# Between layers 1 and 2 of a four-layer sparse graph network: which engine takes roots and norms, in which order the vector work stands, and how the last rows are scaled for layer 3

## The chip, the core and the metric

The kernel runs on one core of one Trainium2 chip. A core has five engines with queues of their own: PE (TensorE, matrix products; PEld is its weight load), DVE (VectorE), ACT (ScalarE), POOL (GpSimd, which here also issues the indirect DMAs) and SP (SyncE, which issues the plain DMAs). Each engine works through its queue in order. What is measured is the device time of one execution in microseconds (us), as the median of several runs.

## What is computed

`x` has 2708 rows of 512 float32 numbers, and `adj` is a 2708 x 2708 matrix with about 0.15% of its entries non-zero, plus its diagonal. Four layers follow one another, each `x = layernorm(x + layer(x, adj))`. The change touches the end of layer 1, the whole of layer 2's scaling, and the way from layer 2 to 3:

```python
# layer 2
mask = incidence_m > 0
head = mask.astype(incidence_m.dtype)
head = head / jnp.maximum(jnp.sqrt(jnp.sum(head * head, axis=-1, keepdims=True)), EPS)
inc = incidence_m + head
edge_fea = inc @ cur
edge_degree = jnp.sum(inc, axis=-1, keepdims=True)
return edge_fea / edge_degree
...
# layer 3
A = adj_matrix + jnp.eye(n, dtype=adj_matrix.dtype)
deg = jnp.sum(A, axis=0)
d = deg ** (-0.5)
d = jnp.where(jnp.isinf(d), 0.0, d)
A = d[:, None] * A * d[None, :]
Hm = A @ H
out = jnp.tanh(Hm @ W.T + b)
```

So layer 2 needs, for every row, one over the root of its count of non-zeros (`inv_norm`) and its row sum; layer 3 needs one over the root of every column sum (`d_inv`), and its gathered rows are already multiplied by it: what layer 3 reads is `y = d_inv * x`.

## The kernel before

The rows are cut into 24 blocks of 113 (the last has 109; `NB`, `R`, `rows(i)`). During layer 0 the kernel finds the non-zeros of each block and keeps them as lists of 4 x 128 edges (`EC` = 4 chunks): source row, row in the block, value. From then on a product `adj @ x` of one block is: four indirect DMAs (`gather`, L600, issued by POOL, 128 rows of 512 numbers each) bring the source rows from a table in HBM to one of three buffers `gath[i % 3]`, and four matrix products (`aggregate`, L613) multiply them by a 128 x 113 spread matrix `s`, which `values` (L1291) makes on DVE. For layer 2 `incidence` (L1564, L1567) makes from `s` the matrix `inc2`. A float32 product appears in the trace as two PE passes.

Each layer ends a block with a layernorm and writes the new rows to the table that the next layer gathers from (`move_rows`, two DMAs on SP): `table[1]` from `norm1`, `table[2]` from `norm2`. A row may be needed by any block, so the first gather of layer 2 waits for the last block's write of `table[1]`, and the first gather of layer 3 for the last write of `table[2]`. PSUM pools are opened anew between the layers (`phase.close()`).

The order of the instructions on every engine is the order of the code: the scheduler is switched off (`manual_schedule`). Around the change that order is, for the last block of layer 1 (i = 23): products `l1s` (`sums1`) and `l1e` (`scored_sums1`); the transpose that brings the column sums in (`source_sums_in`, L1518, with its copy on ACT, L1519); transposes of the first two rows of `inv_norm` (`turn_norm`, L1551); the gates on ACT (`gates1`, L1427, L1428); `gated1` on DVE (L1434 to L1440); the norm of block 22 (`norm1`, L1484, L1487, and its two writes); the loads of layer 3's bias row and of its 1 MB weights on SP; the row norms of the last two blocks (`row_norms`: three small DVE instructions, then `pow` on POOL, L1542); the copies of the two transposed norms on ACT (L1557); 12 unread products that keep PE busy (`keep_warm`, L1527); `both1`, `stats1` and `norm1` of block 23 (`both1`: five DVE instructions and a tanh on ACT, L1464; `stats1`: residual, statistics, then two POOL instructions L1477 and L1478 that make one over the standard deviation; `norm1`: L1484 on DVE, L1487 on ACT, the writes), with five small DVE instructions for layer 2's row sums (L1622 to L1626) between them. Then the column sums: four small DVE instructions (L1629 to L1634) and `pow` on POOL (L1635), the bias row spread over the partitions by a product on PE (L1501) and copied by DVE (L1502), and only then the gathers of layer 2's first two blocks, each with its `values` and `incidence`.

Layer 2's loop gathers block i + 2, multiplies block i, and ends block i - 1 with `stats2` and `norm2`. `norm2` computes mean and scale (L1682, L1683 on DVE), writes `xr = v * scale + bias` (L1686, ACT) and from it `y = xr * d_inv` (L1690, ACT), and sends `y` to `table[2]` (L569, SP).

Of the kernel before, what the change touches and what calls it, by code (L numbers as in the profile page):

```python
# [8 lines left out]
FP = mybir.dt.float32  # L9
AF = mybir.ActivationFunctionType  # L10
ALU = mybir.AluOpType
AX = mybir.AxisListType
P = 128
# [5 lines left out]
R = 113  # L19
# [428 lines left out]
def sparse_stack(  # L448
# [29 lines left out]
    nc = tc.nc  # L478
    N, D = x.shape
    KB = (N + P - 1) // P  # L480
    NF = N // P
    TAIL = N - NF * P
    NB = (N + R - 1) // R
# [17 lines left out]
    xr = xr_cols[:, :, :D]  # L501
# [43 lines left out]
    rowsum, cnt = row_cnt[:, :, 0], row_cnt[:, :, 1]  # L545
# [899 lines left out]
    def both1(i):  # L1445

        r, agg = rows(i), sum_e.pop(i)
        rec = small.tile([P, 1], FP, tag="rec", name=f"rec{i}")
        nc.vector.scalar_tensor_tensor(
            rec[:r, :], agg[:r, 0, 0:1], 1e-5, ediag[:r, i : i + 1], op0=ALU.add, op1=ALU.add  # L1450
        )
        nc.vector.reciprocal(rec[:r, :], rec[:r, :])
        nc.vector.tensor_mul(rec[:r, :], rec[:r, :], gate1.pop(i)[:r, 0:1])
        va = work.tile([P, D], FP, tag="u", name=f"l1a{i}")
        nc.vector.scalar_tensor_tensor(
            halves(va, r), halves(own1.pop(i)[:, :D], r), ediag[:r, i : i + 1],
            agg[:r, :, 1 : H + 1], op0=ALU.mult, op1=ALU.add,
        )
        v = work.tile([P, D], FP, tag="v", name=f"l1v{i}")
        nc.vector.scalar_tensor_tensor(  # L1460
            v[:r, :], va[:r, :], rec[:r, :], vb1.pop(i)[:r, :], op0=ALU.mult, op1=ALU.add
        )

        nc.scalar.activation(v[:r, :], v[:r, :], AF.Tanh, scale=0.5)  # L1464
        v1[i] = v

    def stats1(i):
        r, v = rows(i), v1[i]
        nc.vector.scalar_tensor_tensor(
            v[:r, :], v[:r, :], 0.5, xr[:r, i, :], op0=ALU.mult, op1=ALU.add  # L1470
        )
        stats = small.tile([P, 6], FP, tag="stats", name=f"st_l1_{i}")
        nc.vector.bn_stats(stats[:r, :], v[:r, :])
        mv = small.tile([P, 4], FP, tag="mv4", name=f"mv_l1_{i}")
        nc.vector.bn_aggr(mv[:r, 0:2], stats[:r, :])

        nc.gpsimd.tensor_scalar(mv[:r, 1:2], mv[:r, 1:2], 1e-5, None, op0=ALU.add)  # L1477
        nc.gpsimd.tensor_tensor(mv[:r, 2:3], mv[:r, 1:2], root[:r, :], ALU.pow)  # L1478
        v1[i] = v, mv
# [15 lines left out]
    bg_bc = gpool.tile([P, D], FP, name="bg_bc")  # L1495
    nc.sync.dma_start(out=bg_bc[0:1, :], in_=b_gc[None, :])

    def spread_bias(t):
        ps = ps_sp.tile([P, 4, P], FP, tag="sp", name="bias_rows")
        ps = ps.rearrange("p k r -> p (k r)")  # L1500
        nc.tensor.matmul(ps, lhsT=one_row, rhs=t[0:1, :], start=True, stop=True)  # L1501
        nc.vector.tensor_copy(t, ps)  # L1502
# [13 lines left out]
    def source_sums_in():  # L1516
        ps = ps_sp.tile([P, 4, P], FP, tag="sp", name="deg_s")
        nc.tensor.transpose(ps[:R, 0, :NB], deg_r, ident[:NB, :NB])  # L1518
        nc.scalar.copy(deg[:R, :], ps[:R, 0, :NB])  # L1519

    def keep_warm(pool, tag, shape, n, cols=D):

        o = pool.tile(shape, FP, tag=tag, name="unread")
        if len(shape) == 3:
            o = o.rearrange("p k r -> p (k r)")
        for _ in range(n):
            nc.tensor.matmul(o[:, :cols], lhsT=ident, rhs=bg_bc[:, :cols], start=True, stop=True)  # L1527
# [3 lines left out]
    inv_norm = const.tile([P, NB], FP, name="inv_norm")  # L1531
    nc.vector.tensor_scalar(plus, adiag, 0.0, None, op0=ALU.is_gt)

    def row_norms(at):
        n = at.stop - at.start

        nc.vector.tensor_scalar(
            cnt[:, at], cnt[:, at], 2.0**23, 2.0**23, op0=ALU.add, op1=ALU.subtract
        )
        nc.vector.tensor_add(cnt[:, at], cnt[:, at], plus[:, at])  # L1540
        nc.vector.tensor_scalar(inv_norm[:, at], cnt[:, at], 1e-24, None, op0=ALU.max)
        nc.gpsimd.tensor_tensor(  # L1542
            inv_norm[:, at], inv_norm[:, at], root.to_broadcast([P, n]), ALU.pow
        )

    row_in, inc2 = {}, {}

# [33 lines left out]
    for i in range(NB):  # L1581
        if i + 2 < NB:
            gather1(i + 2)
        sums1(i)
        if i > 0:
            both1(i - 1)
        if 0 < i and i - 1 + NO < NB:
            load_own1(i - 1 + NO)
        if i + 2 < NB:
            values1(i + 2, (0, 1))  # L1590
        scored_sums1(i)
        if i + 1 == NB:
            source_sums_in()
            turn_norm(0)
            turn_norm(1)
        if i + 1 < NB:
            scores1(i + 1)
        if i > 0:
            stats1(i - 1)
        gates1(i)  # L1600
        if i + 2 < NB:
            values1(i + 2, (2, 3))
        gated1(i)
        if i + 1 < NB:
            mask1(i + 1)
        if i > 0:
            norm1(i - 1)
        if i + 1 == NB:
            nc.sync.dma_start(out=b3_bc[0:1, :], in_=b3[None, :])
            nc.sync.dma_start(out=w3_sb, in_=w3T.rearrange("(b p) o -> p b o", p=P))  # L1610
        if i < KB:
            source_sum(i)
        if i == KB:
            source_sums_out()
            row_norms(slice(0, KB))
    row_norms(slice(KB, NB))
    copy_norm(0)
    copy_norm(1)
    keep_warm(ps_sp, "sp", [P, 4, P], 12)
    both1(NB - 1)  # L1620
    stats1(NB - 1)
    nc.vector.tensor_add(rowsum, rowsum, adiag)  # L1622
    nc.vector.tensor_mul(plus, plus, inv_norm)
    nc.vector.tensor_add(plus, plus, adiag)
    nc.vector.tensor_mul(cnt, cnt, inv_norm)
    nc.vector.tensor_add(rowsum, rowsum, cnt)  # L1626
    norm1(NB - 1)

    nc.vector.tensor_add(deg, deg, adiag)  # L1629
    nc.vector.tensor_scalar(deg, deg, 1.0, None, op0=ALU.add)  # L1630
    zero = const.tile([P, NB], FP, name="zero")
    nc.vector.tensor_scalar(zero, deg, 0.0, None, op0=ALU.is_equal)
    d_inv = const.tile([P, NB], FP, name="d_inv")
    nc.vector.tensor_add(d_inv, deg, zero)  # L1634
    nc.gpsimd.tensor_tensor(d_inv, d_inv, root.to_broadcast([P, NB]), ALU.pow)  # L1635
    spread_bias(b3_bc)
    phase.close()
    ps_agg = ctx.enter_context(tc.tile_pool(name="ps_agg2", bufs=2, space=bass.MemoryType.PSUM))
    ps_tr = ctx.enter_context(tc.tile_pool(name="ps_tr2", bufs=1, space=bass.MemoryType.PSUM))
# [4 lines left out]

    for i in range(2):
        gather(gath[i], i, table[1], D)
        incidence(i, values(i))
    nc.vector.reciprocal(rowsum, rowsum)

    nc.vector.tensor_mul(plus, plus, rowsum)  # L1650
# [28 lines left out]
    def norm2(i):  # L1679
        r = rows(i)  # L1680
        v, mv = v2.pop(i)
        nc.vector.reciprocal(mv[:r, 2:3], mv[:r, 2:3])  # L1682
        nc.vector.tensor_scalar(  # L1683
            mv[:r, 3:4], mv[:r, 0:1], mv[:r, 2:3], -1.0, op0=ALU.mult, op1=ALU.mult
        )
        nc.scalar.activation(  # L1686
            xr[:r, i, :], v[:r, :], AF.Identity, bias=mv[:r, 3:4], scale=mv[:r, 2:3]
        )
        y = spool.tile([P, D], FP, tag="y", name=f"y2_{i}")
        nc.scalar.activation(y[:r, :], xr[:r, i, :], AF.Copy, scale=d_inv[:r, i : i + 1])  # L1690
        move_rows(r, lambda a, b: table[2][i * R + a : i * R + b, :], lambda a, b: y[a:b, :])

    own2(0)
# [149 lines left out]
```

## Time and profile before

| | us |
|---|---|
| time, median of 3 runs (1008.12 to 1011.41) | 1010.21 |
| time of the profiled execution | 992.9 |
| its span, first to last instruction | 991.2 |
| PE busy in the span | 899.3 (91%) |
| DVE busy | 686.4 (69%) |
| ACT busy | 530.0 (53%) |
| POOL busy | 473.0 (48%) |

The profiled execution is one execution, and shorter than the runs that were timed without a profile; differences are therefore worked out against its own times and then taken off the median. In its trace layer 1 ends with the `xr` of block 23 at 649.12 us, layer 2's gathers are issued from 653.41 to 783.32 us, layer 3's first gather starts at 796.19 us, and the last products of layer 3 end near the end of the span. In the lines of the trace each row gives the start, the duration, the engine, the line of the code, the operation, `out<-in`, and in brackets how long the engine had been idle and what ended that. SPq and POOLq are the queues in which SP and POOL issue and wait. The table of busy time in stretches lists the stretch, its length, the busy time and instruction count of PE, PEld, DVE, ACT and POOL, the granted PE clock (1.00 is full), the busy share of the DMA engines and their GB/s.

### The profile page before, as it was taken

Reading aid. Unit: us, or ns where it says so; the run is one execution under the profiler, and the core shown is the slowest. Engines: PE = TensorE matmul, PEld = TensorE weight load, DVE = VectorE, ACT = ScalarE, POOL = GpSimd, SP = SyncE. Lnnn points to the kernel's source line nnn. Section 1 sums busy time; section 2 is a strip of 40 time slices with the busy share of each in tenths; the row PEclk is TensorE's granted clock in tenths of the full one; section 3 lists DMA queues with packets and bytes.
Section 4 is the critical chain, followed back from the end, with each engine's and each line's share of the span. In section 5 each row is a group of like instructions: output and inputs, shape, how many; then the busy total and the mean of one; then the engine's idle time right before and its main releaser. Section 6 shows DMA issues by size and latency. Waiting matters only on the chain.

```text
span 991.2 us, 11201 instructions
## 1 busy us (share of the span) xinstructions
PE 899.3 (91%) x2973; PEld 494.5 (50%) x2973; DVE 686.4 (69%) x1803; ACT 530.0 (53%) x1219; POOL 473.0 (48%) x538
## 2 busy tenths in 40 slices
PE   7879999899998999999888888889888889999994
PEld 3335555555555555557666667633333334444441
DVE  7876888788887872138878878858787625655543
ACT  5765767667767664346776777415545412222222
POOL 3313131331313321046666767467777468776640
PEclk8979999999999999989999999989999999999998
DMA  9986877878778544378999998357777556555531
GB/s 237 302 210 173 210 216 195 236 220 223 213 214 219 163 131 123 118 231 294 299 317 283 323 299 279 93 158 211 221 219 211 159 151 181 169 169 163 168 109 32
DMA packets 133516, 201.70 MB, mean 203 GB/s; under 512 B 82456, under 2 KB 82502, under 8 KB 133445
## 3 DMA queue, kind: packets, MB, share of 16 engines
q0 software_dynamic: 36864, 111.73, 38.2%
q1 hardware_dynamic: 96581, 89.18, 31.8%
q8 instruction: 26, 0.43, 0.2%
q14 instruction: 45, 0.37, 0.1%
HBM read 181.83 MB, written 27.80 MB: 211 GB/s over the span
## 4 chain that ended last, share of the span: by engine, by line
PE 50%; DMA 16%; DVE 13%; ACT 10%; issue 6%; POOL 5%; SPq 0%; POOLq 0%; DVEq 0%; ACTq 0%
DMA gath<-table,source 15%; PE o_l L584 13%; PE l3a L613 8%; PE hb L584 5%; PE h L584 5%; PE l0a L613 4%; POOL gath L600 4%; PE l2a L613 4%; ACT s L967 2%; PE unread L1527 2%; DVE where_all L860 2%; ACT nojunk L845 2%; PE l1s L1404 2%; DVE rec_all L858 2%; PE fetched L913 1%
## 5 line engine op out<-in xcount | busy, mean ns | idle before, releaser
L600 POOL DMA_INDIRECT gath<-table,source x288 | 315.9, 1097 | 154.6 <-issue 64.0
L600 POOL DMA_INDIRECT gath<-in_x_dram,source x96 | 97.3, 1014 | 242.4 <-issue 204.5
L1404 PE MATMUL l1s<-gath,s 128*113 128x256 f32 (+3 forms) x384 | 96.6, 407 | 22.6 <-DVE l1b L1434 22.3
L613 PE MATMUL l2a<-gath,s_left 128*113 128x512 f32 (+1 forms) x192 | 95.7, 617 | 16.7 <-DMA gath<-table,source 14.5
L1404 PEld LDWEIGHTS l1s<-gath,s 128*113 128x113 f32 (+1 forms) x384 | 70.9, 189 | 48.4 <-DVE l1b L1434 29.7
L613 PE MATMUL l3a<-gath,s 128*113 128x512 f32 (+1 forms) x192 | 88.4, 602 | 3.6 <-DMA gath<-table,source 3.6
L584 PE MATMUL o_l<-shared,uT_l 128*113 128x512 f32 (+1 forms) x192 | 86.5, 593 | 0.7 <-ACT uT_l L577 0.7
L1414 PE MATMUL l1e<-gath,e 128*113 128x257 f32 (+3 forms) x384 | 87.0, 379 | 0.0
L613 PE MATMUL l0a<-gath,s 128*113 128x512 f32 (+1 forms) x192 | 86.3, 592 | 0.0
L584 PE MATMUL hb<-w_gc_sb,uT_x 128*128 128x512 f32 (+1 forms) x176 | 83.3, 601 | 0.0
L584 PE MATMUL o_l<-w_sb,uw 128*128 128x512 f32 (+1 forms) x176 | 82.4, 612 | 0.2
L584 PE MATMUL h<-w_sa_sb,uT_x 128*128 128x259 f32 (+1 forms) x352 | 81.0, 382 | 1.3 <-ACT w_sa_sb L842 1.3
L584 PEld LDWEIGHTS h<-w_sa_sb,uT_x 128*128 128x128 f32 (+1 forms) x352 | 64.8, 185 | 22.0 <-issue 8.0
L1414 PEld LDWEIGHTS l1e<-gath,e 128*113 128x113 f32 (+1 forms) x384 | 68.1, 177 | 15.2
L1762 ACT ACTIVATE y<-l3v,mv_l 113x512 f32<-113x512 f32 (+1 forms) x24 | 19.5, 813 | 87.3 <-DVE mv_l L1758 87.3
L613 PEld LDWEIGHTS l2a<-gath,s_left 128*113 128x113 f32 (+1 forms) x192 | 30.2, 179 | 71.7 <-DMA gath<-table,source 45.3
L584 PEld LDWEIGHTS o_l<-shared,uT_l 128*113 128x113 f32 (+1 forms) x192 | 33.9, 177 | 48.9 <-issue 47.1
L613 PEld LDWEIGHTS l3a<-gath,s 128*113 128x113 f32 (+1 forms) x192 | 32.6, 180 | 42.2 <-issue 39.3
L613 PEld LDWEIGHTS l0a<-gath,s 128*113 128x113 f32 (+1 forms) x192 | 33.8, 177 | 38.9 <-issue 37.7
L1291 DVE TENSOR_SCALAR s<-niota_r,nrow,edges 128x113 f32<-128x113 f32 x192 | 51.8, 349 | 0.0
L860 DVE FIND_INDEX8 where_all<-rec_all,shared 128x8 uint32<-128x678 f32 (+1 forms) x64 | 51.2, 800 | 0.0
L858 DVE MAX8 rec_all<-shared 128x8 f32<-128x678 f32 (+1 forms) x64 | 50.8, 795 | 0.0
(239 smaller groups left out, 1556.4 us busy)
## 6 DMA issues: line engine op xcount, KB each, us to landing
shared<-in_adj_dram SPq DMA_DIRECT2D x14, 1186.5 KB
table<-st SPq DMA_DIRECT2D x21, 514.5 KB
gath<-in_adj_dram SPq DMA_DIRECT2D x7, 1186.5 KB
shared<-table SPq DMA_DIRECT2D x16, 448.0 KB
gath<-in_x_dram SPq DMA_DIRECT2D x21, 256.0 KB
xi<-in_x_dram SPq DMA_DIRECT2D x23, 224.0 KB
table<-xr SPq DMA_DIRECT2D x23, 224.0 KB
table<-y SPq DMA_DIRECT2D x23, 224.0 KB
```

The costliest lines, as they stand in the source:

```text
L584: nc.tensor.matmul(o, lhsT=uT[:, f, :r], rhs=w[:, f, :], start=(f == 0), stop=(f == DB - 1))
L600: nc.gpsimd.indirect_dma_start(out=g[:, c, :n], out_offset=None, in_=src[:, :], in_offset=bass.IndirectOffsetOnAxis(ap=source[:, i, c : c ...
L613: nc.tensor.matmul(agg[:r, :], lhsT=s[:, c, :r], rhs=g[:, c, off : off + D], start=(c == 0), stop=(c == EC - 1),)
L845: nc.scalar.activation(nojunk, abuf[i % NA].rearrange("p b i -> p (b i)"), AF.Relu, scale=-1.0, accum_out=negs[:, i : i + 1],)
L858: nc.vector.max(out=top, in_=seg)
L860: nc.vector.max_index(out=where_all[:, i, g * 8 : (g + 1) * 8], in_max=top, in_values=seg)
L967: nc.scalar.activation(spread0[i][:, c, :], t, AF.Relu, bias=edges[:, i, c, 1:2], scale=nvalue[:, i, c : c + 1],)
L1291: nc.vector.tensor_scalar(s[:, c, :], niota_r, nrow[:, i, c : c + 1], edges[:, i, c, 1:2], op0=ALU.is_equal, op1=ALU.mult,)
L1404: nc.tensor.matmul(sum_s[i][:r, k, : at.stop - at.start], lhsT=s[:, c, :r], rhs=g[:, c, at], start=(c == 0), stop=(c == EC - 1),)
L1414: nc.tensor.matmul(sum_e[i][:r, k, k : k + at.stop - at.start], lhsT=e[:, c, :r], rhs=g[:, c, at], start=(c == 0), stop=(c == EC - 1),)
L1527: nc.tensor.matmul(o[:, :cols], lhsT=ident, rhs=bg_bc[:, :cols], start=True, stop=True)
L1762: nc.scalar.activation(y[:r, :], v[:r, :], AF.Identity, bias=mv[:r, 3:4], scale=mv[:r, 2:3])
```

## The change

At the end of layer 1:

- `source_sums_in` no longer stands before the gates of block 23; its transpose is issued after `norm1(23)`, its copy moves from ACT to DVE and stands after the first two `incidence`.
- The row norms of blocks 22 and 23 are computed after the column sums, with a square root on ACT and a reciprocal on DVE in place of `pow` on POOL. The five instructions for the row sums follow them.
- `keep_warm` issues 8 products in place of 12. The bias row is spread by PE right after `both1(23)`, and copied by DVE after the first two `incidence`.
- `values` and `incidence` of blocks 0 and 1 come directly after `norm1(23)`.
- `d_inv` takes its root on ACT (`nc.scalar.sqrt`) and its reciprocal on DVE, in place of `pow` on POOL.

At the end of layer 2, for the last block only, `y` is made from `v` directly: one DVE instruction multiplies scale and bias by `d_inv`, `y = v * (scale * d_inv) + bias * d_inv` is the first ACT instruction, and `xr` the second.

```diff
+    def spread_row(t, name):
+        ps = ps_sp.tile([P, 4, P], FP, tag="sp", name=f"rows_{name}")
+        spread_ps[name] = ps = ps.rearrange("p k r -> p (k r)")
+        nc.tensor.matmul(ps, lhsT=one_row, rhs=t[0:1, :], start=True, stop=True)
+
...
     def source_sums_in():
         ps = ps_sp.tile([P, 4, P], FP, tag="sp", name="deg_s")
         nc.tensor.transpose(ps[:R, 0, :NB], deg_r, ident[:NB, :NB])
-        nc.scalar.copy(deg[:R, :], ps[:R, 0, :NB])
+        return ps
...
-        nc.gpsimd.tensor_tensor(
-            inv_norm[:, at], inv_norm[:, at], root.to_broadcast([P, n]), ALU.pow
-        )
+        if on_pool:
+            nc.gpsimd.tensor_tensor(
+                inv_norm[:, at], inv_norm[:, at], root.to_broadcast([P, n]), ALU.pow
+            )
+        else:
+            nc.scalar.sqrt(inv_norm[:, at], inv_norm[:, at])
+            nc.vector.reciprocal(inv_norm[:, at], inv_norm[:, at])
...
         if i + 1 == NB:
-            source_sums_in()
             turn_norm(0)
             turn_norm(1)
...
-    row_norms(slice(KB, NB))
     copy_norm(0)
     copy_norm(1)
-    keep_warm(ps_sp, "sp", [P, 4, P], 12)
+    keep_warm(ps_sp, "sp", [P, 4, P], 8)
     both1(NB - 1)
+    spread_row(b3_bc, "b3")
     stats1(NB - 1)
-    nc.vector.tensor_add(rowsum, rowsum, adiag)
-    nc.vector.tensor_mul(plus, plus, inv_norm)
-    nc.vector.tensor_add(plus, plus, adiag)
-    nc.vector.tensor_mul(cnt, cnt, inv_norm)
-    nc.vector.tensor_add(rowsum, rowsum, cnt)
     norm1(NB - 1)
-
+    deg_ps = source_sums_in()
+    inc_s = [values(0)]
+    incidence(0, inc_s[0])
+    inc_s.append(values(1))
+    incidence(1, inc_s[1])
+    nc.vector.tensor_copy(b3_bc, spread_ps["b3"])
+
+    nc.vector.tensor_copy(deg[:R, :], deg_ps[:R, 0, :NB])
     nc.vector.tensor_add(deg, deg, adiag)
...
     nc.vector.tensor_add(d_inv, deg, zero)
-    nc.gpsimd.tensor_tensor(d_inv, d_inv, root.to_broadcast([P, NB]), ALU.pow)
-    spread_bias(b3_bc)
+    nc.scalar.sqrt(d_inv, d_inv)
+    row_norms(slice(KB, NB), False)
     phase.close()
...
     for i in range(2):
         gather(gath[i], i, table[1], D)
-        incidence(i, values(i))
+    nc.vector.tensor_add(rowsum, rowsum, adiag)
+    nc.vector.tensor_mul(plus, plus, inv_norm)
+    nc.vector.tensor_add(plus, plus, adiag)
+    nc.vector.tensor_mul(cnt, cnt, inv_norm)
+    nc.vector.tensor_add(rowsum, rowsum, cnt)
+    nc.vector.reciprocal(d_inv, d_inv)
     nc.vector.reciprocal(rowsum, rowsum)
...
+        y = spool.tile([P, D], FP, tag="y", name=f"y2_{i}")
+        if i + 1 == NB:
+
+            di = d_inv[:r, i : i + 1]
+            nc.vector.tensor_mul(mv[:r, 0:2], mv[:r, 2:4], di.to_broadcast([r, 2]))
+            nc.scalar.activation(
+                y[:r, :], v[:r, :], AF.Identity, bias=mv[:r, 1:2], scale=mv[:r, 0:1]
+            )
         nc.scalar.activation(
             xr[:r, i, :], v[:r, :], AF.Identity, bias=mv[:r, 3:4], scale=mv[:r, 2:3]
         )
-        y = spool.tile([P, D], FP, tag="y", name=f"y2_{i}")
-        nc.scalar.activation(y[:r, :], xr[:r, i, :], AF.Copy, scale=d_inv[:r, i : i + 1])
+        if i + 1 < NB:
+            nc.scalar.activation(y[:r, :], xr[:r, i, :], AF.Copy, scale=d_inv[:r, i : i + 1])
```

More of the change, by code (lines that the diff above doesn't have):

```diff
@@ L1496, in sparse_stack @@
     nc.sync.dma_start(out=bg_bc[0:1, :], in_=b_gc[None, :])
+    spread_ps = {}
+    def spread_row(t, name):
+        ps = ps_sp.tile([P, 4, P], FP, tag="sp", name=f"rows_{name}")
+        spread_ps[name] = ps = ps.rearrange("p k r -> p (k r)")
+        nc.tensor.matmul(ps, lhsT=one_row, rhs=t[0:1, :], start=True, stop=True)
     def spread_bias(t):
@@ L1532, in sparse_stack, with row_norms @@
     nc.vector.tensor_scalar(plus, adiag, 0.0, None, op0=ALU.is_gt)
-    def row_norms(at):
+    def row_norms(at, on_pool=True):
         n = at.stop - at.start
```

## The prediction

> **What bounds the kernel now.** I read the chain of waits on the page first, then the table of stretches for layer 2, then one line's view of the gathers, and last the timeline at both ends of layer 2, where the change lies. The chain is mixed:
>
> ```profile
> PE 50%; DMA 16%; DVE 13%; ACT 10%; issue 6%; POOL 5%; SPq 0%; POOLq 0%; DVEq 0%; ACTq 0%
> ```
>
> Whole-span shares don't answer for one stage. For layer 2, from its first gather to its last, the stretch, the gathers in it and PE's waits are:
>
> ```profile
> 653.41:783.32 129.91, 113.73 (x262) 42.07 (x261) 97.32 (x266) 61.73 (x113) 100.94 (x96) 0.99 0.72 208
> ...
> L600 POOL DMA_INDIRECT gath<-table,source x96: 994/998/1444, 653.4 to 782.3; - x96
> ...
> PE l2a L613 <- DMA gath<-table,source: 14.5, 23, 1.8
> ```
>
> 96 gathers in 129.91 us are 1.353 us each: 100.94 / 96 = 1.05 us busy and 0.30 us between two, at every one of them. POOL issues without a gap, PE waits for data 23 times: layer 2 is as long as POOL's 96 gathers, and its end moves with their start. The reader's question is what releases the first gather:
>
> ```profile
> 638.88 0.13 DVE L1424 TENSOR_TENSOR gate<-l1s,gates 109x2 f32<-109x2 f32 x1
> ...
> 640.17 0.18 ACT L1519 COPY deg<-deg_s 113x24 f32<-113x24 f32 x1 [2.88 <-PE deg_s L1518]
> 640.25 0.21 ACT L1427 ACTIVATE gate<-gate 109x2 f32<-109x2 f32 x1
> 640.35 0.15 ACT L1428 COPY row_cnt<-l1s 109x2 f32<-109x2 f32 x1
> 640.54 0.75 DVE L1434 SCALAR_TENSOR_TENSOR l1b<-w_sb,adiag,l1s 109x512 f32<-109x512 f32 x1 [1.53 <-ACT row_cnt L1428]
> ...
> 648.05 0.21 DVE L1484 TENSOR_SCALAR mv_l<-mv_l 109x1 f32<-109x1 f32 x1 [0.37 <-POOL mv_l L1478]
> 648.30 0.82 ACT L1487 ACTIVATE xr<-l1v,mv_l 109x512 f32<-109x512 f32 x1 [2.98 <-DVE mv_l L1484]
> ...
> 649.07 4.17 POOL L1635 TENSOR_TENSOR d_inv<-d_inv,root 128x24 f32<-128x24 f32 x1 [1.06 <-DVE d_inv L1634]
> 649.14 0.76 SPq L569 DMA_DIRECT2D table<-xr  x2
> ...
> 653.41 1.17 POOL L600 DMA_INDIRECT gath<-table,source  x1 [0.17 <-issue]
> ...
> 660.18 5.38 PE L613 MATMUL l2a<-gath,s_left 128*113 128x512 f32 x8 [2.03 <-DVE s_left L1567]
> ```
>
> See three things: the gates (ready at 639.01) stand behind the column sums' copy on ACT; the last rows are written at 649.14; and POOL's `pow` of `d_inv` ends at 653.24, just ahead of the gather. The first product at 660.18 waits for DVE, behind the unread products and the bias row (the chain of waits goes that way), but POOL meets that product again only at the 13th gather, at 669.86, which needs the buffer that l2a(0) leaves at 665.56: 4.3 us of slack. So the 16.4 us of the chain from the unread products to l2a(0) (643.74 to 660.18) aren't what is to be had. At the other end:
>
> ```profile
> 790.96 0.21 DVE L1683 TENSOR_SCALAR mv_l<-mv_l 109x1 f32<-109x1 f32 x1
> ...
> 791.21 0.81 ACT L1686 ACTIVATE xr<-l2v,mv_l 109x512 f32<-109x512 f32 x1 [0.48 <-DVE mv_l L1683]
> 792.06 0.72 ACT L1690 ACTIVATE y<-xr,d_inv 109x512 f32<-109x512 f32 x1
> 792.81 0.75 SPq L569 DMA_DIRECT2D table<-y  x2
> 796.19 1.00 POOL L600 DMA_INDIRECT gath<-table,source  x1 [12.88 <-issue]
> ```
>
> Everything there is in series, and layer 3 behind it is PE's (175.81 of 189.00 us busy from 801 to 990), so it moves as a whole.
>
> **What the Trainium skill says.** "PSUM — Partial Sum Buffer", section on bank collisions: two engines' accesses to one bank are kept apart, reads too. This fits L1434, which reads what L1428 reads and starts 0.04 us after it; so ACT's delay becomes DVE's. "ScalarE: Activation LUTs", section "What ACT_TABLE_LOAD costs": 1.283 us for the load, and about 1.38 us of drain. The trace has 1.28 us, at 666.84, with no drain that shows. "DMA: Bandwidth & Descriptors", section "Anatomy of one DMA": most of a write's fixed 2 us comes after the last byte. The trace agrees in part: the `y` write is issued at 792.81, its packets end near 794.6, its landing is 795.10. "TensorE: Matmul & The Clock Gate", Part 1: the clock is decided over free-running windows of 3.4 us; here the changes at 644.3, 647.7, 661.2, 664.6, 801.1 and 804.5 us lie on such a grid.
>
> **The change, part by part.**
>
> *Gates first.* L1427 starts some 0.16 us after L1424, as one block earlier (631.48 to 631.64): 639.04 in place of 640.25, so 1.21 us; L1434 starts at 639.33. L1449 still finds its input, since l1e(23) ended at 639.93.
>
> *Row norms of blocks 22 and 23 moved back.* L1537, L1540, L1541 leave the front of `both1`: L1484 to L1449 was 642.00 to 642.59; the instruction after L1484 started 0.12 us behind it, so 0.47 us. `both1(23)` is 1.68 us earlier. The ACT queue ahead of its tanh (L1443, L1487, two copies) ends at 643.85 - 1.21 = 642.64, before the tanh at 643.00. The row-sum instructions between L1475 and L1484 were covered by POOL's L1477 and L1478; without them DVE waits there. So `xr(23)` goes from 648.30 to 646.62, its write from 649.14 to 647.46.
>
> *`pow` off POOL.* Gone from in front of the gather. What is next late is the write's landing. POOL's queue shows the semaphores of that write from 651.5 to 652.1 and a last one at 652.7 before the pow ended: without it the gather would have started near 652.9, not 653.41. So this alone is worth 0.5 us, not 4.17. Write issue to gather: 3.76 us here by that count, 3.38 us at the end of layer 2 (792.81 to 796.19). I take the middle, 3.57: first gather at 651.03. The ends are 650.84 and 651.22, and later if the 1 MB weight load is in the way: its packets run until 649.35, the write's from 649.9. It is issued 1.21 us earlier and ends near 648.15, while the write's packets would start near 648.25. The gap shrinks from 0.55 to 0.1 us; a collision costs up to about 0.5. **Start of layer 2: 2.4 us earlier** (1.7 to 2.6).
>
> *What was added must stay inside POOL's slack.* `incidence` of blocks 0 and 1: before, 657.70 to 662.37, 4.67 us; now from 646.55 to about 651.2. PE: the unread products start 1.2 us earlier, at 642.53, and 8 fewer passes at 0.43 us leave 8.8 of 12.26 us: 651.4; bias row 1.06: 652.4; column sums 0.3. DVE copies both by 653.4 (0.69 + 0.18), then four instructions of the d_inv group, three of the norms, ACT's two roots, a reciprocal, five row sums, two reciprocals and five more at about 0.2, with two crossings: near 657.7. `values` and `incidence` of block 2, 2.4 us: 660.1, needed when gather(2) has landed, near 651.0 + 10.5 + 3.5 = 665. l2a(0) runs at the pace of its gathers (landing 3.5 us after the start): 654.5 to about 659.4, against 667.5 when POOL wants the buffer. Cover 5 to 8 us; beyond it, each us costs one. Cost nil. The root's table load, 1.28 us, moves from 666.84 to behind `xr(23)`, at 647.4, where ACT waits for DVE until 654: nil; a drain would be covered as well. SP's order is the same. One load of the set serves as before, since `xr` and `y` followed the root without another.
>
> *Last rows.* DVE's multiply adds about 0.19 us (790.77 to 790.96 is the step between two such), `y` with a bias takes 0.81, not 0.72, and `xr`'s 0.85 step is behind it: 0.85 - 0.19 - 0.09 + 0 = 0.57; the multiply is of the L1683 kind, so between 0.15 and 0.25: **0.6 us** (0.5 to 0.65). `xr(23)` itself is wanted only at layer 3's end.
>
> Sum: 2.4 + 0.6 = 3.0 us; profiled execution 992.9 - 3.0 = 989.9; median 1010.21 - 3.0 = 1007.2. What the timed runs have over the profiled one, 17.3 us, I carry over unchanged.
>
> **Rivals.**
>
> *The landing eats the gain.* Weight load and last write meet, and the gather starts at 651.5 to 652: 1.4 to 1.9 us, with the last rows 2.0 to 2.5: 1007.9. For it: the 0.1 us gap. Against: the same engines reached 410 GB/s, so a collision is short.
>
> *PE's clock helps at layer 3.* Before, PE idled 3.29 us ahead of layer 3 and ran at 0.50 from 801.13 to 804.5; l3a(0) ended at 805.63, when its last gather (800.10 + 3.6 = 803.7) would have allowed 804.7. The gap shrinks to 2.7 us; if it no longer trips the clock, 0.9 us more: 1006.3. Against: the windows run freely, so mostly one still falls in the gap.
>
> *Slower: PE is cold in layer 2.* With 8 unread products and a l2a(0) that trickles in with the gathers, the clock stays at 0.50. A block then takes 2 x (3.44 + 0.86 + 0.26) = 9.1 us of PE against 4 x 1.353 = 5.41 of POOL, 3.7 us lost per block once the 8 us of slack are gone; three cold blocks use up the slack and the gain of 3.0 us, five cost (5 x 3.7 - 8) - 3.0 = 7.5 net: 1017.7. Against: at 661.2 the clock fell and was back at 664.6, and PE's new gap, about 1.5 us, is shorter than the 3 us before.
>
> *No effect.* Some other limit of layer 2 holds its end, time 1010. Against: no gap in POOL in 130 us.
>
> **How the numbers follow.** Forecast 0.52, landing 0.22, clock 0.17, slower 0.06, no effect 0.03. The forecast's own range is 1005.6 to 1008.8, from the bounds (2.2 to 3.25) and about 1.3 us for the scatter of a median out of 1008.12 to 1011.41. With the rivals but the slower one: 1004.2 to 1010.4. The bound of 0.3%, about what a measurement can tell from no change, is 3.03 us, where the forecast lies itself: faster 0.47 (half the forecast, nearly all of the clock's case, a tenth of the landing's, and a little for what I count too low), same 0.45, slower 0.08.
>
> **What would show it.** In the new trace: `xr(23)`'s write 1.6 to 1.8 us earlier relative to the end of l1e(23); no POOL work between L1478 and the first gather; that gather 3.4 to 3.8 us after the write; l2a(0) released by DMA, not DVE; 96 gathers in 129 to 131 us; `y` ahead of `xr` and the step L1683 to SP 1.2 us in place of 1.85. It is wrong if POOL shows gaps in layer 2, if the gather stands over 4 us behind the write, or if PE's clock is at 0.50 beyond two windows there.

## The result, and the profile after

| | before | after | ratio, 95% interval |
|---|---|---|---|
| median of 12 runs each, us | 1010.0 | 1007.78 | 0.9987 [0.9966, 1.0007] |
| the same two kernels on a second chip (54 and 10 runs) | 992.13 | 988.98 | 0.9955 [0.9938, 0.9972] |
| on a third chip (63 and 22 runs) | 991.24 | 987.98 | 0.9974 [0.9963, 0.9985] |

The first comparison alone is no more than "within 0.3%". The other two belong to the experiments, and say that the changed kernel is faster, by 2.6 us (1.5 to 3.7) on the third chip. The ratio is estimated from all the runs; it isn't the quotient of the two medians, whose differences are 2.2, 3.2 and 3.3 us. The profiled execution of the changed kernel took 1005.37 us (span 1003.2) against 992.9 before (span 991.2). Some executions, of either kernel (b_inc below), have stretches in which little but DMA moves; the profile of before shows an execution without them, the profile of after one with them. So stages are compared one by one, never the two spans.

From the timeline of the changed kernel, the end of layer 1 (start, duration, engine, line, operation):

```profile
640.40 0.13 DVE L1424 TENSOR_TENSOR gate<-l1s,gates 109x2 f32<-109x2 f32 x1
640.56 0.20 ACT L1427 ACTIVATE gate<-gate 109x2 f32<-109x2 f32 x1 [1.75 <-DVE gate L1424]
640.67 0.14 ACT L1428 COPY row_cnt<-l1s 109x2 f32<-109x2 f32 x1
640.85 0.75 DVE L1434 SCALAR_TENSOR_TENSOR l1b<-w_sb,adiag,l1s 109x512 f32<-109x512 f32 x1 [0.32 <-ACT row_cnt L1428]
...
648.13 0.82 ACT L1487 ACTIVATE xr<-l1v,mv_l 109x512 f32<-109x512 f32 x1 [2.98 <-DVE mv_l L1484]
648.97 0.76 SPq L569 DMA_DIRECT2D table<-xr  x2
653.11 1.17 POOL L600 DMA_INDIRECT gath<-table,source  x1 [5.26 <-PE unread L1534]
```

The start of L1424 serves as the zero of time, as it doesn't depend on how long the earlier layers took. Before, L1427 came 1.37 us behind its start, now 0.16. The last rows are written 8.57 us after L1424 in place of 10.26, and the first gather follows after 12.71 in place of 14.53: 1.82 us earlier. But the step from write to gather, 4.14 us, is hardly shorter than the 4.27 of before, although no `pow` stands on POOL any more. At the end of layer 2:

```profile
797.07 0.21 DVE L1700 TENSOR_SCALAR mv_l<-mv_l 109x1 f32<-109x1 f32 x1
797.31 0.16 DVE L1707 TENSOR_TENSOR mv_l<-mv_l,d_inv 109x2 f32<-109x2 f32 x1
797.51 0.81 ACT L1708 ACTIVATE y<-l2v,mv_l 109x512 f32<-109x512 f32 x1 [0.67 <-DVE mv_l L1707]
798.23 0.80 ACT L1711 ACTIVATE xr<-l2v,mv_l 109x512 f32<-109x512 f32 x1
801.74 1.00 POOL L600 DMA_INDIRECT gath<-table,source  x1 [12.22 <-issue]
```

From the mean's instruction (L1683 before, L1700 now) to layer 3's first gather: 5.23 us before, 4.67 now, 0.56 us gained. Between the two, layer 2 in the table of busy time in stretches (columns as before), first in this profile, then in one of the changed kernel on the third chip:

```profile
653.11:789.60 136.49, 114.25 (x252) 44.23 (x251) 94.33 (x268) 58.27 (x112) 99.89 (x96) 0.91 0.68 198
```

```profile
650.19:780.50 130.31, 114.30 (x256) 40.94 (x255) 95.58 (x270) 61.01 (x114) 101.13 (x96) 0.97 0.72 208
```

POOL's busy time is the same 100 to 101 us in both; in the first, its 96 gathers have 7.6 us of gaps, in the second none beyond the 0.30 us between any two. The waits of the first, over layer 2 (waiting instruction, what ended the wait, us in total, times, longest):

```profile
ACT row_in L1568 <- remote: 28.4, 5, 11.6
...
PE unread L1534 <- remote: 11.3, 3, 6.4
...
DVE l2v L1685 <- remote: 10.0, 2, 7.1
...
POOL gath L600 <- remote: 2.4, 3, 1.8
```

"Remote" is another core or a queue that the profile doesn't know; this program has one core, and the undisturbed profiles, that of before among them, have no such row. One such stretch beside the 12 us ahead of it:

```profile
700.00:712.00 12.00, 11.32 (x26) 3.67 (x25) 7.67 (x22) 5.20 (x11) 9.26 (x10) 1.00 0.77 222
712.30:718.60 6.30, 0.00 (x0) 0.00 (x0) 0.00 (x0) 0.28 (x1) 3.57 (x5) 0.85 0.71 217
```

PE, its weight loads and DVE start nothing for 6.3 us, while DMA goes on at 217 GB/s; then all go on within 0.1 us of one another. The 12.0 us between the two spans are: 1.52 ahead of L1424, -1.82 at the start of layer 2, +6.51 in its gathers, -0.10 from the last gather to the mean, -0.56 at the last rows, +6.48 in layer 3. Only the second and the fifth are the change's.

### The profile page after: what moved, and what is told of

Its sections match the earlier page's. It is cut to its first block, busy times and chain, and to the rows that moved or that the text cites. A ratio compares the mean times of both kernels' runs of the same rounds, so it can differ in the third digit from the quotient of the medians.

```text
span 1003.2 us, 11186 instructions
## 1 busy us (share of the span) xinstructions
PE 901.4 (90%) x2965; PEld 498.4 (50%) x2965; DVE 686.7 (68%) x1807; ACT 529.9 (53%) x1220; POOL 467.7 (47%) x536
## 4 chain that ended last, share of the span: by engine, by line
PE 52%; DVE 17%; ACT 10%; DMA 8%; issue 7%; POOL 3%; another core or an unknown queue 2%; SPq 0%; POOLq 0%; DVEq 0%; ACTq 0%
PE o_l L584 12%; PE l2a L613 8%; PE l3a L613 8%; DMA gath<-table,source 6%; PE hb L584 5%; PE h L584 5%; PE l0a L613 4%; PE unread L1534 2%; ACT s L967 2%; DVE where_all L860 2%; ACT nojunk L845 2%; POOL gath L600 2%; PE fetched L913 2%; DVE rec_all L858 1%
## 5 line engine op out<-in xcount | busy, mean ns | idle before, releaser
L1404 PE MATMUL l1s<-gath,s 128*113 128x256 f32 (+3 forms) x384 | 94.3, 400 | 23.3 <-DVE l1b L1434 22.9
L613 PE MATMUL l3a<-gath,s 128*113 128x512 f32 (+1 forms) x192 | 90.5, 616 | 2.8 <-DMA gath<-table,source 2.8
L613 PEld LDWEIGHTS l2a<-gath,s_left 128*113 128x113 f32 (+1 forms) x192 | 34.3, 192 | 55.8 <-issue 40.5
L1534 PE MATMUL unread<-bg_bc,ident 128*128 128x512 f32 x80 | 42.9, 652 | 20.1 <-remote 11.3
L1761 DVE SCALAR_TENSOR_TENSOR l3v<-o_l,d_inv,b_bc 113x512 f32<-113x512 f32 (+1 forms) x25 | 18.1, 729 | 57.6 <-PE o_l L584 50.2
```

Of the source, the lines that this page charges most:

```text
L613: nc.tensor.matmul(agg[:r, :], lhsT=s[:, c, :r], rhs=g[:, c, off : off + D], start=(c == 0), stop=(c == EC - 1),)
L1404: nc.tensor.matmul(sum_s[i][:r, k, : at.stop - at.start], lhsT=s[:, c, :r], rhs=g[:, c, at], start=(c == 0), stop=(c == EC - 1),)
L1761: nc.vector.scalar_tensor_tensor(v[:r, at], o[:r, at], d_inv[:r, i : i + 1], b3_bc[:r, at], op0=ALU.mult, op1=ALU.add,)
```

## The experiments

Twelve runs in three groups of four, each group on one chip beside the kernel before. Stages from the traces, in us; "write", "gather" and "l2a(0)" are the last write of layer 1's rows, layer 2's first gather and its first product, "95" is from the first gather of layer 2 to the start of the last, and "rows" from the last block's mean to layer 3's first gather. A star marks profiles with stretches that stand still.

| kernel | L1424 to write | write to gather | L1424 to gather | L1424 to l2a(0) | 95 | rows |
|---|---|---|---|---|---|---|
| before | 10.26 | 4.27 | 14.53 | 21.30 | 128.91 | 5.23 |
| b_same | 10.24 | 4.27 | 14.51 | 21.28 | 128.98 | 5.22 |
| b_root | 10.26 | 3.45 | 13.71 | 21.11 | 128.43 | 5.24 |
| b_inc * | 10.25 | 4.31 | 14.56 | 18.12 | 136.87 | 5.22 |
| b_inc2 | 10.24 | 4.32 | 14.56 | 18.21 | 128.62 | 5.24 |
| b_add2 | 10.25 | 4.65 | 14.90 | 20.24 | 130.09 | 5.24 |
| after * | 8.57 | 4.14 | 12.71 | 16.24 | 135.42 | 4.67 |
| a_same | 8.57 | 4.18 | 12.75 | 16.21 | 127.37 | 4.67 |
| a_same2 | 8.57 | 4.15 | 12.72 | 16.32 | 129.10 | 4.67 |
| a_no_y * | 8.57 | 4.20 | 12.77 | 16.25 | 137.41 | 5.23 |
| a_sums_first * | 9.78 | 4.24 | 14.02 | 17.52 | 135.88 | 4.68 |
| a_w3_late | 8.58 | 3.41 | 11.99 | 15.92 | 127.39 | 4.67 |
| a_inc_late * | 8.57 | 3.44 | 12.01 | 19.80 | 136.40 | 4.66 |
| a_inc_late2 | 8.57 | 3.47 | 12.04 | 21.23 | 129.94 | 4.67 |

### First group: both kernels once more, the weight load, the root alone (second chip, before 992.13)

**b_same** is the kernel before, with no edit.

> The kernel before, once more: what a second profile of it looks like. Theory (stalls come and go): the profile of before (span 991.2 us) was an uncommonly quiet one; its timed runs lie near 1010, so most of its executions should show, as the changed kernel's profile does (673 to 684, 712 to 718, 820 to 830 us), stretches in which ACT, DVE and PE stand still for 3 to 12 us together in layers 2 and 3, with a span of 1000 to 1010 and POOL's gathers of layer 2 taking 133 to 140 us in place of 129.9. Rival (the change made these stalls): the span is again 990 to 994 with no such stretch. Either way: first gather 14.5 us after the last gates' DVE instruction (L1424), as before (638.88 to 653.41), ratio 1.000.

0.9994 [0.9983, 1.0005], span 994.3, and no stretch that stands still. That expectation failed on this chip: the quiet profile of before was no exception here, it is the rule. The stretches belong to a chip or an execution.

**a_same** is the changed kernel, with no edit.

> The changed kernel, once more. Theory: the first gather again 12.5 to 12.9 us after L1424 (12.71 in its first profile, 14.53 before), and L1700 to the first gather of layer 3 4.6 to 4.75 us (4.67; 5.23 before), so 2.4 us of the forecast 3.0 in every execution; ratio 0.997 to 0.998 with stalls in other places or of other length. Rival (the stalls belong to the changed code): stalls at the same instructions as in its first profile, ratio 0.999 to 1.003.

0.9955 [0.9938, 0.9972]; span 986.9, nothing stands still. So the change didn't bring the stretches either. 12.75 to the first gather repeats after's 12.71.

**a_w3_late**: in the changed kernel, layer 3's 1 MB weight load is issued behind the last write, not ahead of it.

```diff
-            nc.sync.dma_start(out=w3_sb, in_=w3T.rearrange("(b p) o -> p b o", p=P))
...
     norm1(NB - 1)
+    nc.sync.dma_start(out=w3_sb, in_=w3T.rearrange("(b p) o -> p b o", p=P))
```

> The changed kernel with the 1 MB load of layer 3's weights issued behind the last write of layer 1 and not ahead of it. Theory (the write queues behind the load's packets, landing 0.6 us later than it could): write issue to first gather 3.4 to 3.7 us, not 4.14; the first gather 12.0 to 12.3 us after L1424; ratio 0.0005 under the changed kernel's. Rival (landing time has nothing to do with the load): still 4.0 to 4.2 us. A price could be later landings of the first gathers beside the load, 1 to 3 us, which the slack of 8 us at the 13th gather should hide.

Write to gather falls from 4.18 to 3.41 us; 0.9956 [0.994, 0.9973], the same as a_same. At first this reads as proof that load and write collide in the changed kernel. The third group shows that it isn't.

**b_root**: in the kernel before, only the root of `d_inv` goes to ACT, with its reciprocal on DVE.

```diff
-    nc.gpsimd.tensor_tensor(d_inv, d_inv, root.to_broadcast([P, NB]), ALU.pow)
+    nc.scalar.sqrt(d_inv, d_inv)
+    nc.vector.reciprocal(d_inv, d_inv)
```

> The kernel before with one part alone: the root of the column sums on ACT and a reciprocal on DVE, not pow on POOL. Theory (POOL's 4.17 us hid the landing of the last write, of which only the tail was exposed): first gather 0.5 us nearer to L1424, 13.9 to 14.1 us in place of 14.53; ratio 0.9995. Rival (POOL's pow is what delayed layer 2): 3 to 4 us nearer, ratio 0.996.

The timeline of ACT in b_root, where the write is issued at 651.57 and the gather starts at 655.02:

```profile
650.73 0.82 ACT L1487 ACTIVATE xr<-l1v,mv_l 109x512 f32<-109x512 f32 x1 [2.98 <-DVE mv_l L1484]
651.56 1.28 ACT L1635 ACT_TABLE_LOAD   x1
652.85 0.22 ACT L1635 ACTIVATE d_inv<-d_inv 128x24 f32<-128x24 f32 x1
```

Table load and root lie inside the write's 3.45 us. The gather starts 0.8 us earlier than before: of POOL's 4.17 us only that was on the path. The time, 0.9995 [0.9981, 1.0009], is a gain of 0.5 us, within a gain of 1.9 and a loss of 0.9, and doesn't contradict it.

### Second group: single parts (a chip like the first, before 1011.52)

**b_inc**: the kernel before with the first two `incidence` ahead of the bias row, and 8 unread products.

```diff
-    keep_warm(ps_sp, "sp", [P, 4, P], 12)
+    keep_warm(ps_sp, "sp", [P, 4, P], 8)
...
+    for i in range(2):
+        incidence(i, values(i))
     spread_bias(b3_bc)
...
         gather(gath[i], i, table[1], D)
-        incidence(i, values(i))
```

> The kernel before with one part alone: values and incidence of blocks 0 and 1 ahead of the bias row, 8 unread products in place of 12. Theory (POOL sets layer 2's pace): the first gather stays 14.5 us behind L1424, the first product of layer 2 comes 3 to 5 us earlier than its 21.3, and the time is unchanged but for what a less crowded start saves POOL: the 95 gathers from the first to the last start take 127.4 us, as in the changed kernel, not 128.9, ratio 0.9985. Rival 1 (only the start of the gathers counts, the 1.5 us are chance): 128.4 to 129.0 us, ratio 1.000. Rival 2 (the chain of waits is right, the first product sets layer 2): 3 us or more, ratio 0.996.

l2a(0) comes 3.2 us earlier, the gathers don't: 1.0000 [0.9978, 1.0023]. With its stretches the 95 gathers take 136.87 us, so that 127.4 and 128.4 us can't be told apart here; b_inc2 does that.

**a_inc_late**: the changed kernel with `values` and `incidence` of blocks 0 and 1 back behind their gathers, 12 unread products, and the bias row after the column sums.

```diff
+    keep_warm(ps_sp, "sp", [P, 4, P], 12)
     both1(NB - 1)
-    spread_row(b3_bc, "b3")
...
-    inc_s = [values(0)]
-    incidence(0, inc_s[0])
-    inc_s.append(values(1))
-    incidence(1, inc_s[1])
...
         gather(gath[i], i, table[1], D)
+        incidence(i, values(i))
```

> The changed kernel with that part undone: 12 unread products, bias row behind them, incidence of blocks 0 and 1 behind the bias row. Theory: first gather still 12.7 us behind L1424, first product at 20 to 21 us, and the 95 gathers back at 128.4 to 129.0 us: ratio to the kernel before 0.997 where the changed kernel has 0.9955. Rival 1: 127.4 us, 0.9955 as it was. Rival 2 (the first product sets layer 2): the gain goes but for the 0.6 us of the last rows, 0.999.

l2a(0) is 3.6 us later than in the changed kernel, and the time is as good: 0.9969 [0.9948, 0.999]. The first product doesn't set layer 2. The first gather was forecast as before, at 12.7 us, and came at 12.01; the third group has the reason. The 95 gathers hold stretches here too, so their forecast isn't tested.

**a_no_y**: the changed kernel with the last rows as before, `xr` first and `y` from it (the `y` part of the diff undone).

> The changed kernel without the last part: y of the last block again from xr. Theory: L1683's successor to the first gather of layer 3 is 5.23 us, not 4.67, and nothing else moves: ratio to before 0.9961 where the changed kernel has 0.9955. Rival (PE's clock at the start of layer 3 eats or doubles it): layer 3 from its first gather to the end is longer or shorter than 194.5 to 195.5 us by over 0.5 us.

"Rows" goes back to 5.23, and the stages up to the first gather stay; 0.9968 [0.995, 0.9986]. The 0.56 us are below what this timing resolves. Layer 3 has stretches in this profile (202.53 us), so the rival isn't tested by it.

**a_sums_first**: the changed kernel with the column sums' transpose and their copy on ACT ahead of the last gates again.

```diff
         if i + 1 == NB:
+            deg_ps = source_sums_in()
+            nc.scalar.copy(deg[:R, :], deg_ps[:R, 0, :NB])
             turn_norm(0)
...
-    deg_ps = source_sums_in()
...
-    nc.vector.tensor_copy(deg[:R, :], deg_ps[:R, 0, :NB])
```

> The changed kernel with the transpose of the column sums and its copy on ACT put back ahead of the last gates. Theory (ACT's copy holds the gates, and DVE waits for the gates' copy): L1424 to the last write 9.7 to 9.8 us in place of 8.57, the first gather 13.6 to 14.0 us behind L1424 in place of 12.75, as a later write is further from the 1 MB load; ratio to before 0.9966. Rival (DVE's wait is for something else): 8.57 us.

The write is 9.78 us after L1424, 1.21 later than in the changed kernel: that is the gates' part to the hundredth. The 0.48 us that stay gained (10.26 to 9.78) are by difference the row norms'; they weren't moved alone. The write stands further from the weight load than in the changed kernel, and write to gather is 4.24 us all the same, so that part of the forecast failed. So did its ratio: 1.0001 [0.9979, 1.0023], not 0.9966; the 0.5 + 0.55 us that this trace gains would be 0.999, which the interval holds.

All four profiles of this group stand still for some stretches, b_inc's with the order of before among them.

### Third group: is layer 2 itself shorter, and why do some gathers take longer (third chip, before 991.24)

In a_same layer 2's 95 gathers were 1.5 us shorter than before. Either the earlier incidence does that, or it is scatter.

**b_inc2** and **a_inc_late2** are b_inc and a_inc_late again, **a_same2** the changed kernel.

> The kernel before with only the first two incidences moved ahead of the last norm (and 8 unread products). Theory: the earlier incidence runs ahead of the gathers, meets fewer of them, and that is the 1.5 us by which layer 2's 95 gathers are shorter in the changed kernel: 127.4 us from first to last where no stretch of the layer stands still, ratio 0.9985. Rival, the 1.5 us come from where the gathers happen to fall against DVE's instructions once their start has moved: 128.4 to 129 us, ratio 1.000.

> The changed kernel with the first two incidences back behind the gathers. Theory of the earlier incidence: 128.9 us from first to last gather of layer 2, ratio 0.9976 (start of layer 2 by 1.8 us and last rows by 0.56 are kept). Rival, the fall of the gathers: somewhere from 127.4 to 129 us, ratio 0.996 to 0.9976.

> The changed kernel as it is, beside the other three on one chip: 127.4 us from first to last gather of layer 2 if no stretch of the layer stands still, ratio 0.9955 to 0.997.

b_inc2: 128.62 and 1.0008 [0.9995, 1.0021]. a_inc_late2: 129.94 and 0.9963 [0.995, 0.9975]. a_same2: 129.10 and 0.9974 [0.9963, 0.9985]. One and the same kernel has 127.37 in one execution and 129.10 in another; the 1.5 us were scatter, and the theory of the earlier incidence falls.

a_inc_late2 settled the other question. Its write lands early, as in a_w3_late, though the weight load stands ahead of it as in the changed kernel. The transfers from 0.85 to 2.9 us after the issue of the last write, in 40 slices (busy tenths, GB/s), with the queues (packets, MB, share of 16 engines); first a_same2, then a_inc_late2:

```profile
DMA  9798947957996752125000200020001011000000
GB/s 560 240 240 200 280 120 200 280 200 280 320 360 200 240 200 80 40 80 120 0 0 0 40 0 0 0 40 0 0 0 40 0 40 40 0 0 0 0 0 0
...
q1 hardware_dynamic: 133, 0.21, 37.0%
q8 instruction: 1, 0.02, 2.9%
```

```profile
DMA  9999979989999694752100000000000000000000
GB/s 320 360 320 280 360 240 280 320 320 280 280 360 400 240 320 160 280 200 80 40 0 0 0 0 0 0 0 0 0 0 0 0 0 0 0 0 0 0 0 0
...
q1 hardware_dynamic: 172, 0.28, 42.1%
```

In a_inc_late2 more bytes are under way, the weight load is still among them, and all is done after 20 slices (1.0 us). In a_same2 it is one packet at a time after 19 slices, until slice 34: 0.7 us later. And a_same2 has a packet that the other lacks: an instruction fetch, which starts 0.85 to 0.90 us after the write's issue and holds one of the 16 DMA engines for 0.96 us (2.9% of 16 engines in 2.05 us). POOL's wait for the write is seen in its queue, from the write to the gather; a_same2 above, a_inc_late2 below (min, median and max in ns, first and last start):

```profile
L600 POOLq EVENT_SEMAPHORE  x6: 17/43/744, 648.4 to 650.0; - x6
```

```profile
L600 POOLq EVENT_SEMAPHORE  x6: 17/43/43, 650.1 to 651.0; - x6
```

In a_inc_late2 no semaphore takes over 0.043 us; in a_same2 one takes 0.744. With the single packets above: one of the transfer's parts is late by 0.7 us, the rest is in time. That the parts are counted singly and the slowest decides is what the Trainium skill says ("DMA: Bandwidth & Descriptors", section "Why a DMA increments its semaphore by 16 and not by 1"), and this agrees. Over all profiles:

| instruction fetch against the write's issue | write to gather |
|---|---|
| +0.75 to +1.0 us: after, a_same, a_same2, a_no_y, a_sums_first | 4.14 to 4.24 |
| ahead of it (b_root by at most 0.25 us, a_w3_late by 1.5 to 1.75), or none in the 3 us around it (a_inc_late, a_inc_late2) | 3.41 to 3.47 |
| `pow` on POOL until 4.10 to 4.13 us after the write: before, b_same, b_inc, b_inc2 | 4.27 to 4.32 |
| the same `pow`, no fetch in the 3 us around the write's issue: b_add2 | 4.65 |

No edit moved the fetch by itself, but executions did. One and the same kernel has it 0.1 us after the write's issue in before and 10.3 us after it in b_same; 10.3 us after it in a_inc_late and 4.0 us ahead in a_inc_late2; 0.5 us after it in b_inc and 3.4 us ahead in b_inc2. In this last pair `pow` holds the gather, but POOL's queue shows the write; b_inc above, b_inc2 below:

```profile
L600 POOLq EVENT_SEMAPHORE  x7: 17/42/388, 650.1 to 651.9; - x7
```

```profile
L600 POOLq EVENT_SEMAPHORE  x8: 17/30/43, 651.7 to 653.6; - x8
```

The packets give the measure. In all eight profiles whose fetch is still under way 1.1 us or more after the write's issue, the write's last packet starts 0.84 us after the fetch ends (us from the write's issue):

| profile | fetch ends | last packet of the write starts |
|---|---|---|
| b_root | 1.12 | 1.96 |
| before, b_inc | 1.42, 1.43 | 2.26, 2.27 |
| after, a_same2, a_same | 1.80, 1.81, 1.85 | 2.64, 2.65, 2.69 |
| a_no_y, a_sums_first | 1.87, 1.91 | 2.71, 2.75 |
| none under way then: b_same, b_inc2, a_inc_late, a_inc_late2 | - | 1.90 to 1.92 |
| the same, and the weight load behind the write: a_w3_late | - | 1.96 |

So the write's last part waits for the fetch, with the same code and with other code. By this a_w3_late gained because its fetch came ahead of the write, not because the load was out of the way. Which engine's instructions the fetch brings isn't seen.

A fetch isn't the only thing that can hold the last part. In b_add2 none is near, and yet the write lands later than in any other profile:

```profile
L600 POOLq EVENT_SEMAPHORE  x6: 17/43/1266, 651.6 to 653.7; - x6
```

There packets follow one another singly, 0.08 us apart, until the last of the weight load's sixteen closing packets (4 bytes each) at 2.78 us after the write's issue; six more and the write's own last packet, at 3.26, come behind it. The gather starts 0.54 us after `pow` has ended, where before it was 0.17. So here one late part of the weight load held the write, which in a_inc_late2 it overlapped without harm. Why that part was late isn't known.

**b_add2**: the kernel before with the two-input instruction of `incidence` doubled; the second, a maximum, leaves the values as they are.

```diff
         nc.vector.tensor_add(inc, inc, s)
+        nc.vector.tensor_tensor(inc, inc, s, op=ALU.max)
```

> The kernel before, in which the incidence of layer 2 does its two-input DVE instruction twice per block (the second, a maximum of the same two tiles, leaves the values as they are). If the gathers that take 1.1 to 1.5 us on POOL in place of 1.0 are held up by a DVE instruction with two inputs in SBUF, their excess over 1.0 us, 4.9 us in the kernel before, about doubles (8 to 10 us), and first to last gather of layer 2 goes from 128.9 to about 133 us: ratio about 1.004. Rival, the long gathers come from the transfers or the memory: the excess stays at 4.4 to 5.1 us, and the ratio at 1.000, since DVE has the room (97 of 130 us busy).

Neither came. Excess 5.9 us, 95 gathers in 130.09, 1.0004 [0.9989, 1.0019]. The unaltered changed kernel has 3.5 us of excess in one execution and 5.2 in another, so 1.0 us more than before's 4.9 says little. (The longer "write to gather", 4.65, is the late write above.) What the timeline of before shows is an overlap:

```profile
677.95 0.63 DVE L1567 TENSOR_TENSOR s_left<-s_left,s 128x452 f32<-128x452 f32 x1
678.04 1.41 POOL L600 DMA_INDIRECT gath<-table,source  x1 [0.31 <-PE l2a L613]
679.58 0.75 DVE L1668 SCALAR_TENSOR_TENSOR l2v<-l2a,row_cnt,l2v 113x512 f32<-113x512 f32 x1 [1.00 <-PE l2a L613]
679.75 1.00 POOL L600 DMA_INDIRECT gath<-table,source  x1 [0.30 <-PE l2a L613]
```

Of the 33 gathers that overlap an L1567 within their first us, 17 take over 1.04 us; of the 63 others only the first does. The add at 677.95 goes with 1.41 us. But doubling the adds raised the excess by no more than two executions of one kernel differ. Nor was the test as strong as it was meant to be: each second add stands directly behind its first, so that 40 gathers meet an add in place of 33, and the excess per such gather is 0.15 us in both. The cause isn't settled.

## Why the prediction came out as it did

The number held, 1007.2 forecast and 1007.78 measured, but the likeliest case was not the one that happened. By its own steps:

- **Gates first, 1.21 us, and row norms moved back, 0.47.** Both right: 1.21 and 0.48 by a_sums_first, 1.69 together, in all seven profiles that have both parts.
- **Landing, 3.57 us from write to gather.** The term that was mis-sized: 4.14 to 4.18 in the changed kernel, which is "over 4 us behind the write", one of the forecast's own signs of being wrong. Its middle of two readings was near where nothing disturbs the write (3.41 to 3.47), and so was the list of what is late next after the `pow`. The disturber was named wrongly: the weight load did no harm in the changed kernel, even overlapped with the write (a_inc_late2), though it can (b_add2), and what held its last part, an instruction fetch that starts 0.84 to 0.89 us after the issue, wasn't looked for. The profile of before has such a fetch from 0.1 to 1.42 us after the write's issue, and one semaphore of the write took 0.36 us there, so that the reading of 3.76 us held 0.3 us of it already; reading the queues there by kind would have shown it. The start of layer 2 gained 1.8 us in place of 2.4, inside the 1.7 to 2.6 of the bounds and the 1.4 to 1.9 of the landing rival, which has the size right and, for the changed kernel, the cause wrong. So the time came out near the forecast with the rival's size of gain, on a scatter that would have let either pass: that is in part luck.
- **`pow` alone, 0.5 us.** b_root gives 0.82, as its fetch ends early enough to hold the write by only 0.06 us. "Not 4.17" was the point, and it held.
- **Added work at no cost.** Held. `incidence` of blocks 0 and 1 ran from 0.96 us before the write to 3.76 after it, forecast -0.91 to 3.74. l2a(0) was released by DMA, and the margin is large: 3.1 to 4.9 us more or less at l2a(0) changed no time (b_inc, b_inc2, a_inc_late, a_inc_late2). The table load came directly behind `xr(23)` and cost nothing, with no drain to be seen. From the timeline of a_inc_late2, where DVE is late again and still nothing is lost:

```profile
660.37 5.78 PE L613 MATMUL l2a<-gath,s_left 128*113 128x512 f32 x8 [1.87 <-DVE s_left L1578]
```

- **Last rows, 0.6 us.** Measured 0.56; the worked term was 0.57.
- **Layer 2 is as long as POOL's gathers.** Right where nothing stands still: 130.31 us from first gather to last end, no gap. It is no law: with the stretches POOL has gaps of 7.6 to 11.2 us in layer 2, and the sentence "it is wrong if POOL shows gaps" would have condemned a premise that holds.
- **PE's clock at layer 3.** It happened once: in a_w3_late the clock stays full there (1.00 from 797 to 814 us, 0.90 in a_same), and from its first gather to the end layer 3 takes 194.31 us. With a mean clock of 0.90 or 0.91 in its first 18 us it takes 194.48 to 194.99 (before, b_root, b_inc2, a_same, a_same2, a_inc_late2), with 0.81 it takes 195.47 and 195.49 (b_same, b_add2). So the rival is worth 0.2 to 0.7 us, not 0.9. PE's gap did shrink from 3.3 to 2.7 us; that the 0.81 fell only on quiet profiles with the order of before, 2 of 5 against 0 of 4, is too few to count as an effect of the change. (Two of the clock's changes that the forecast reads at 644.3 and 647.7 us stand at 644.11 and 647.53 in the trace; they too are 3.4 us apart.)
- **PE cold in layer 2; no effect.** Neither. In a_same2 the clock over layer 2 is 0.97; and the start of the gathers moves the end.

Together the traces give 1.8 + 0.56 = 2.4 us. The three timed comparisons give 1.3, 4.5 and 2.6 us by their ratios (0.0013 x 1010, 0.0045 x 992, 0.0026 x 991) and 2.2, 3.2 and 3.3 by their medians. The first and the third interval contain 2.4; the second, 2.8 to 6.2, doesn't quite, and no stage in its trace that repeats accounts for the rest. Carrying 17.3 us over unchanged from profile to timed runs did no harm: with either kernel the runs of the slower occasions lie 18 to 20 us above those of the others.

No version that beats the changed kernel is proved. a_inc_late and a_w3_late start layer 2 another 0.7 us earlier in the trace; a_inc_late2's median is 0.65 us under a_same2's, with overlapping intervals, and a_w3_late's ratio equals a_same's.

## What to carry to other kernels

A step that ends in a DMA write ends with the slowest of its parts: ahead of pricing it, list what else is on the DMA engines in that us, by kind of queue: instruction fetches, and loads that aren't done yet. When work leaves an engine, the gain is the time until the next thing that is late, here 0.8 us of a 4.17 us instruction. And before a difference of 1 to 2 us in a stage is given a cause, profile the unchanged kernel twice.

## What the runs showed of the hardware

- An instruction fetch of about 0.02 MB holds one DMA engine for 0.95 to 1.6 us, and the last packet of a 218 KB write that it meets starts 0.84 us after its end, in eight of eight profiles; that is 0.06 to 0.85 us later than without it. The Trainium skill calls the cost of such a fetch mostly hidden ("Runtime: NRT & Kernel Launch", section "Instruction fetch mechanics"); here a write's last part waits behind it.
- Where that fetch falls isn't set by the code alone: it stood 0.84 to 0.89 us after the write's issue in all three profiles of the changed kernel, but 0.1 and 10.3 us after it in two of the kernel before. So it isn't shown that moving the DMA issue in a_w3_late is what moved it.
- One of the sixteen parts of a 1 MB load was late by itself, by 2.0 us against the next latest, and the write behind it waited (b_add2).
- On two of the four occasions the kernels ran some 18 to 20 us longer (1010 against 991 to 992), in either order of the code, and five of the profiles have stretches of 3 to 12 us in layers 2 and 3 in which PE, DVE and ACT stand still together while DMA goes on. Their cause stays open.
- A gather's issue takes 1.00 us on POOL mostly, but 1.05 to 1.47 us for 15 to 23 of 96 in the undisturbed profiles, and the sum of that differs by 1.7 us between two executions of one kernel.
